# Four layers in one program: output projection folded into the value weights, shorter copies of the folded-in rows in two convolutions, and two sets of loads moved

## Chip, cores and metric

One core of a Trainium2 chip runs the whole program. The metric is the device time of one execution in microseconds. The core has five engines with a queue each: TensorE (PE, with its weight loads shown apart as PEld), VectorE (DVE), ScalarE (ACT), GpSimd (POOL) and SyncE (SP). SP and ScalarE issue the DMAs here. Numbers like L778 are lines of the kernel before.

## What is computed

The input is one image of 48 channels and 128x128 pixels (N = 16384 pixels). Four layers follow each other, each adding its result to its input after a group normalisation `_gn` (16 groups of 3 channels):

```
x = x + L0(_gn(x))   # attention over all 16384 pixels, one head of 48 channels
x = x + L1(_gn(x))   # four recurrent sweeps: down, up, right, left
x = x + L2(_gn(x))   # patch convolution with a product in the frequency domain
x = x + L3(_gn(x))   # state space scan over 4096 tokens of 192 values
```

- L0: a 1x1 convolution to 144 channels and a 3x3 depthwise one give q, k, v; q and k are normalised to length one; `softmax(q k^T * temperature) v` for every pixel; then a 48x48 projection of the result.
- L1: each row (then column) is its input plus a 5-tap convolution of the row before it, 508 steps that depend on each other.
- L2: a 1x1 convolution to 288 channels and a 3x3 depthwise one; q and k of each 8x8 patch are multiplied in the frequency domain, normalised over channels, multiplied by v and projected to 48 channels.
- L3: tokens of 2x2 pixels; B, C and the step sizes are matrix products of the tokens; a linear recurrence over the 4096 tokens for 192x192 states; output per token.

## The kernel before

Two image buffers, `xa` and `xb`, stay in on-chip memory (128 partitions, channels on partitions 0 to 47) and change roles between layers. `tile_kernel` (L1503) loads the image in 8 pieces on SP, then calls `attention`, `sweeps`, `patch_conv`, `image_out` and `scan`. Each takes its buffers from pools that it gives back at its end; a buffer that lies on given-back memory waits for that memory's last users.

The order on each engine is fixed when the program is built. `InOrder` (L38) keeps the operations of one wrapper in the order in which they are written; what is issued past it may be ordered otherwise by the builder. A queue's instructions are taken strictly in turn, so a DMA on SP that waits keeps those behind it waiting. Eight semaphores are shared by all DMAs in rotation, so a DMA is issued only when the one eight places before it has landed.

**Both convolutions** (L166 to L233, L741 to L818) fold the depthwise 3x3 kernel into the 1x1 weights (`packed_weights`, L100): a product of both for each of 9 taps, summed by matmuls. Partitions are packed so that three matmuls (one for each horizontal shift) cover most of it: partitions 0 to 47 (48 in the patch convolution, with a row of ones) hold image row y, partitions 64 on hold row y+1, and the gaps between hold a part of the channels of row y+2. The remaining channels of row y+2 are copied three times, with the three shifts, into a buffer `rest`, once at partition 0 and once at 64, and a fourth matmul takes those. Two neighbouring outputs (two halves of eight rows in attention, even and odd rows in the patch convolution) take the copy at 0 and the copy at 64, so that two small matmuls can lie side by side on TensorE. Each of the two copies holds all rows.

In attention a `band` is 16 rows: normalised by VectorE, one copy of the whole to the upper partitions (L181), two for the gaps (L183), six for `rest` (L191), all on SP, two bands in flight. In the patch convolution `fill` (L760) does the same for 8 rows with L765, L768 and L778, `rest` in a ring of three buffers; the first fill puts its `rest` copies on ScalarE's queue. TensorE works in groups g of 4 rows: `columns` (the three shifts), later `others` (the `rest` matmul), then the transforms, `turn`, `leave` and `count`.

**Attention's loop** (`attend`, L303). For each chunk of 512 queries (32 chunks), 64 steps: `scores` makes s = k^T q in four quarter matmuls on both halves of the keys, ScalarE exponentiates, `sums` adds v e into `acc` two steps later. Channel 32 of v is a column of ones, so `acc` also holds the softmax denominators. `Finish` copies `acc` out and adds the two halves (L361). At step 6 of the next chunk `result` multiplies by `proj` (L365), which also spreads the denominators over 48 partitions, and divides and adds the input. `attend_shifted` is for large temperatures and doesn't run here.

**Sweeps** load their weights `w` and `wi` (L573, L575) at their beginning. **`image_out`** (L1537) stores the image to `x3` in device memory in 8 pieces and forms the last normalisation's statistics; the scan reads `x3` back, for its first chunk in `first` (L1042), where ScalarE and VectorE then normalise it into `xn`. The scan itself runs over 4 chunks of 1024 tokens with 288 scans each on VectorE (L1478) and as many products on GpSimd (L1471).

Of the kernel before, what the change touches and what calls it, by code (L numbers as in the profile page):

```python
# [26 lines left out]
C = 48  # L27
H = W = 128
# [85 lines left out]
def attention(ctx, tc, xq, other, x1, const, ins):  # L114
# [11 lines left out]
    v = other[:, HALF:N].rearrange("p (t c) -> p t c", c=64)  # L126


    proj = kv.tile([128, 64 + C], F32, name="proj")
    nc.vector.memset(proj, 0.0)  # L130
    for b in (0, 64):
        nc.sync.dma_start(proj[b : b + GAP, 0:C], ins["l0_proj"])
        nc.vector.memset(proj[b + 32 : b + 33, 64:], 1.0)
    temp = kv.tile([128, 1], F32, name="temp")
# [8 lines left out]
    with ExitStack() as a:  # L143
# [8 lines left out]
        wt = packed_weights(nc, wp, "wt", ins["l0_w"], ins["l0_dw"], 192)  # L152

        for i in range(NQ):
            nc.vector.bn_stats(st[:, i, :], xq[0:C, i * CH : (i + 1) * CH])
# [5 lines left out]
        bands = [wp.tile([128, R + 2, S], F32, name=f"band{i}") for i in range(2)]  # L161
        rests = [wp.tile([128, R, S], F32, name=f"rest{i}") for i in range(2)]
        for t in bands + rests:
            nc.gpsimd.memset(t, 0.0)

        def band(b):  # L166

            t, e = bands[b % 2], rests[b % 2]  # L170
            first = b * R - 1
            lo, hi = max(first, 0), min(first + R + 2, H)
            normalise(
                nc,
                t[0:C, lo - first : hi - first, 1 : W + 1],
                rows(xq[0:C, lo * W : hi * W]),
                stats,
            )
            if b == NB - 1:
                nc.gpsimd.memset(t[0:C, hi - first : hi - first + 1, :], 0.0)  # L180
            nc.sync.dma_start(t[64 : 64 + C, 0 : R + 1], t[0:C, 1 : R + 2])  # L181
            for n in range(2):
                nc.sync.dma_start(  # L183
                    t[64 * n + C : 64 * n + 64, 0:R], t[16 * n : 16 * n + 16, 2 : R + 2]
                )
            flat = t.rearrange("c h w -> c (h w)")
            long = R * S - 2
            for n in range(2):
                for dx in range(3):
                    at = 64 * n + 16 * dx  # L190
                    nc.sync.dma_start(  # L191
                        e.rearrange("c h w -> c (h w)")[at : at + 16, 0:long],
                        flat[32:C, 2 * S + dx : 2 * S + dx + long],
                    )
            return t, e

        def conv(p, pv, te, y):
# [12 lines left out]
            def rest(out, n, c):  # L210
                at = 64 * n
                pe.matmul(
                    rows(out),
                    lhsT=wt[at : at + C, 3, c],
                    rhs=e[at : at + C, y + 4 * n : y + 4 * n + 4, 0:W],
                    start=False,
                    stop=True,
                )
# [16 lines left out]
        def take(t0, p, pv):  # L235
# [36 lines left out]
            nc.gpsimd.memset(k[kb + 32 : kb + 33, tk : tk + 2 * CH], 1.0)  # L272
            nc.gpsimd.memset(v[:, t0 // 128 : t0 // 128 + 8, 32:33], 1.0)
            return left
# [21 lines left out]
    with tc.If(small <= bits) as near:  # L296
        attend(tc, xq, k, v, x1, proj, absT, st, ins)
    with near.Else():
        attend_shifted(tc, xq, k, v, x1, proj, absT, ident, st, ins)


@with_exitstack
def attend(ctx, tc, xq, k, v, x1, proj, absT, st, ins):  # L303

# [45 lines left out]
    class Finish:  # L350


        def __init__(self, c, acc):
# [5 lines left out]
            act.copy(o, acc)  # L359
            self.o = sp.tile([128, CH], F32, name="osum")  # L360
            nc.vector.tensor_add(self.o, o[:, 0], o[:, 1])  # L361

        def result(self):
            p = ps_s.tile([128, 2, CH], F32, name="s")[0 : 64 + C, 0, :]
            pe.matmul(p, lhsT=proj, rhs=self.o, start=True, stop=True)  # L365
            y = sp.tile([64 + C, CH], F32, name="y")
            act.copy(y, p)
            rec = sp.tile([C, CH], F32, name="rec")
            nc.vector.reciprocal(rec, y[64 : 64 + C])  # L369
            nc.vector.tensor_mul(rec, y[0:C], rec)  # L370
            nc.vector.tensor_add(xq[0:C, self.cols], rec, self.xres)
            nc.vector.bn_stats(st[:, self.c, :], xq[0:C, self.cols])
            nc.sync.dma_start(x1[:, self.cols], xq[0:C, self.cols])
# [22 lines left out]
@with_exitstack  # L396
def attend_shifted(ctx, tc, xq, k, v, x1, proj, absT, ident, st, ins):

# [14 lines left out]
    for i in range(0, HALF, 2048):  # L413
        nc.vector.tensor_copy(k16[:, i : i + 2048], k[:, i : i + 2048])

    class Shift:
# [46 lines left out]
    class Finish:  # L463
# [10 lines left out]
        def result(self):  # L474
            p = ps_1.tile([128, CH], F32, name="pmisc")
            nc.tensor.matmul(p[0 : 64 + C], lhsT=proj, rhs=self.o, start=True, stop=True)
            rec = sp.tile([C, CH], F32, name="rec")
# [76 lines left out]
def sweeps(ctx, tc, xq, other, x1, const, ins):  # L554
# [15 lines left out]


    w = pool.tile([128, 3, 3, K], F32, name="w")
    nc.sync.dma_start(w, ins["l1_w"])  # L573
    wi = pool.tile([128, 3, K], F32, name="wi")
    nc.sync.dma_start(wi, ins["l1_wi"])  # L575
    mask = pool.tile([128, L], F32, name="mask")
# [118 lines left out]
@with_exitstack  # L695
def patch_conv(ctx, tc, xq, other, const, ins):

# [42 lines left out]


    K1 = C + 1
    SP = W + 2
# [8 lines left out]
    stats = group_stats(nc, wp, ps_f, const, name="f")  # L752
    flat = xp.rearrange("c h w -> c (h w)")
    rests = [wp.tile([128, RN, SP], F32, name=f"rest{i}") for i in range(3)]

    def rest(y):

        return rests[(y + 1) // RN % 3][:, (y + 1) % RN, 0:W]

    def fill(r, queue=nc.sync):  # L760
        inside = xp[0:64, 1 + r : 1 + RN + r, 1 : W + 1]
        nc.gpsimd.memset(inside[32:64], 1.0)
        normalise(nc, inside[0:C], rows(xq[0:C, r * W : (r + RN) * W]), stats)
        new = slice(r + 1, r + 1 + RN)
        nc.sync.dma_start(xp[64 : 64 + K1, r : r + RN, :], xp[0:K1, new, :])  # L765
        lo, hi = max(r - 1, 0), H if r + RN == H else r - 1 + RN
        for n in range(2):
            nc.sync.dma_start(  # L768
                xp[64 * n + K1 : 64 * n + 64, lo:hi, :],
                xp[M * n : M * n + M, lo + 2 : hi + 2, :],  # L770
            )
        e = rests[r // RN % 3].rearrange("c h w -> c (h w)")
        size = KR // 3
        long = RN * SP - 2
        for n in range(2):
            for dx in range(3):
                at = 64 * n + size * dx
                queue.dma_start(  # L778
                    e[at : at + size, 0:long],
                    flat[2 * M : K1, (r + 1) * SP + dx : (r + 1) * SP + dx + long],  # L780
                )
# [116 lines left out]
    def count(g):  # L898
        dve.bn_stats(const["st"][:, g, :], xq[0:C, g * CH : (g + 1) * CH])

    NG = H // G
    fill(0, act)
    fill(RN)
# [41 lines left out]
def scan(ctx, tc, x3, const, ins, out):  # L945
# [72 lines left out]
    def prepare(ci):  # L1018
# [9 lines left out]
        def first():  # L1028
# [6 lines left out]
            for part in range(NP):  # L1035
                us.append(ap.tile([C2, 2, L], F32, name="xn"))
                src = x3[:, part * NR * W : (part + 1) * NR * W].rearrange(
                    "c (i a w) -> a c i w", a=2, w=W
                )
                raw = rows(ct[0:C2, part, :])  # L1040
                for i in range(2):
                    nc.sync.dma_start(raw[i * C : (i + 1) * C], src[i])  # L1042
            for part, x in enumerate(us):
                xi = rows(ct[0:C2, part, :]).rearrange("c i (j b) -> c i j b", b=2)
                xo = x.rearrange("c b (i j) -> c i j b", j=64)
# [457 lines left out]
def tile_kernel(ctx: ExitStack, tc: tile.TileContext, ins: dict, out: bass.AP):  # L1503
# [4 lines left out]
    x1 = dram.tile([C, N], F32, name="x1")  # L1508
    x3 = dram.tile([C, N], F32, name="x3")
    with ExitStack() as image:  # L1510
        xp = image.enter_context(tc.tile_pool(name="image", bufs=1))

        xa = xp.tile([128, W * (W + 6)], F32, name="xa")
        xb = xp.tile([128, (H + 6) * (W + 6)], F32, name="xb")
        for i in range(0, N, 2048):
            nc.sync.dma_start(xa[0:C, i : i + 2048], ins["x"][:, i : i + 2048])
        attention(tc, xa, xb, x1, const, ins)
        sweeps(tc, xa, xb, x1, const, ins)
        patch_conv(tc, xb, xa, const, ins)
        image_out(tc, xb, x3, const)  # L1520
    scan(tc, x3, const, ins, out)
# [14 lines left out]
@with_exitstack  # L1536
def image_out(ctx, tc, xq, x3, const):  # L1537

    nc = tc.nc
    pool = ctx.enter_context(tc.tile_pool(name="io", bufs=1))  # L1540
    psum = ctx.enter_context(tc.tile_pool(name="io_ps", bufs=1, space=PSUM))
    for i in range(0, N, 2048):
        nc.sync.dma_start(x3[:, i : i + 2048], xq[0:C, i : i + 2048])
    token_stats(tc, pool, psum, const)
# [171 lines left out]
```

## Time and profile before

The median of three executions is 7664.13 us (7662.93 to 7669.04). The profiled execution took 7668.22 us; its span, from the first to the last instruction, is 7666.4 us.

| Stage | us from the start | length |
|---|---|---|
| image load, statistics, first band | 0 to 43 | 43 |
| attention: convolution | 43 to 254 | 211 |
| attention: loop over chunks | 254 to 3817 | 3563 |
| last result, statistics, first rows of the sweeps | 3817 to 3841 | 24 |
| sweeps | 3841 to 4508 | 667 |
| patch convolution, up to its second group | 4508 to 4550 | 42 |
| patch convolution, rest | 4550 to 4925 | 375 |
| store of the image, loads and first products of the scan | 4925 to 4941 | 16 |
| scan | 4941 to 7666 | 2725 |

Over the whole span TensorE is busy for 6186.0 us, ScalarE 4405.6, VectorE 3353.1, GpSimd 2793.6. These sums say little, because the stages have different limits; the stretches below are by stage. In lines of the timeline the first two numbers are start and length in us, then engine, line, operation, what is written and read with its shape, and how many instructions were merged; the bracket tells how long the engine stood idle before, and what ended that. L48 is the line of the `InOrder` helper, so such operations are told apart by their buffers.

### The profile page before, as it was taken

What the parts mean: (1) busy time and instruction counts of PE and PEld (TensorE: products, weight loads), DVE (VectorE), ACT (ScalarE), POOL (GpSimd) and SP (SyncE); (2) the same over time, 40 slices, a digit from 0 to 9 for tenths busy, and PEclk for the clock granted to TensorE, in tenths of its full rate; (3) what the DMA queues carried; (4) which work ended last, traced back from release to release, by engine and by line L of the source; (5) the groups of instructions that cost most, each with busy time, mean ns of one, the idle gap of its engine ahead of it and who ended that gap; (6) DMA issues with size and microseconds to landing.
All of it is one profiled execution on the core that took longest, in us unless ns stands there. A gap on an engine that the chain in (4) does not pass through costs nothing. (4 is left out here: it accounts for less than half of the span.)

```text
span 7666.4 us, 202951 instructions
## 1 busy us (share of the span) xinstructions
PE 6186.0 (81%) x93744; PEld 3145.7 (41%) x93744; DVE 3353.1 (44%) x2435; ACT 4405.6 (57%) x4864; POOL 2793.6 (36%) x573
## 2 busy tenths in 40 slices
PE   7999999999999999999988879745545555554555
PEld 2333333333333333333367755434434333434444
DVE  8300000000000000000022234489999999999998
ACT  2566666666666666666625003366666666666665
POOL 1000000000000000000000022299999999999998
PEclk9999999999999999999999999866767666776666
DMA  5000000000000000000000001166556566666776
GB/s 76 10 3 3 3 2 3 3 3 2 3 3 2 3 3 3 2 3 3 6 1 17 1 27 50 31 168 165 158 161 164 152 161 155 164 158 162 181 178 152
DMA packets 167594, 488.77 MB, mean 64 GB/s; under 512 B 33568, under 2 KB 51968, under 8 KB 163984
## 3 DMA queue, kind: packets, MB, share of 16 engines
q1 hardware_dynamic: 160584, 469.79, 24.4%
q8 instruction: 736, 12.06, 0.7%
q10 hardware_dynamic: 6152, 5.92, 0.3%
q14 instruction: 122, 1.00, 0.0%
HBM read 428.82 MB, written 22.02 MB: 59 GB/s over the span
## 5 line engine op out<-in xcount | busy, mean ns | idle before, releaser
L48 ACT ACTIVATE e<-s,absT 128x1024 f32<-128x1024 f32 x2048 | 2279.4, 1115 | 1215.1 <-PE s L48 1215.0
L1471 POOL TENSOR_TENSOR h<-du,bt 128x3072 f32<-128x3072 f32 (+1 forms) x386 | 2559.8, 6670 | 94.5 <-DMA du<-rep 77.4
L48 PE MATMUL s<-xa,xb 49*64 49x512 f32 x16384 | 2127.7, 589 | 10.6 <-DVE xb L266 10.6
L48 PE MATMUL acc<-e,xb 64*64 64x512 f32 x16384 | 2123.6, 588 | 0.0
L1478 DVE TENSOR_TENSOR_SCAN h<-dA,carry,h 128x1024 f32<-128x1024 f32 x864 | 1939.8, 2324 | 46.1 <-ACT dA L48 31.2
L48 ACT ACTIVATE dA<-dt,a 128x1024 f32<-128x1024 f32 x1152 | 1287.2, 1118 | 873.8 <-DVE h L1478 864.6
L48 PE MATMUL y<-h,cw 128*32 128x48 f32 x49152 | 892.0, 245 | 930.6 <-issue 486.6
L361 DVE TENSOR_TENSOR osum<-o 128x512 f32<-128x512 f32 x32 | 22.2, 693 | 3114.2 <-ACT o L48 3114.2
L593 POOL MEMSET xa<- 48x128 f32 x1 | 0.3, 324 | 3560.3 <-PE acc L48 3560.3
L48 PEld LDWEIGHTS y<-h,cw 128*32 128x32 f32 x49152 | 802.8, 139 | 1059.7 <-issue 650.7
L48 PEld LDWEIGHTS s<-xa,xb 49*64 49x64 f32 x16384 | 624.8, 132 | 1152.1 <-issue 603.7
L48 PEld LDWEIGHTS acc<-e,xb 64*64 64x64 f32 x16384 | 627.1, 132 | 1135.0 <-issue 1112.4
L1478 DVE TENSOR_TENSOR_SCAN h<-dA,h 128x1024 f32<-128x1024 f32 x288 | 636.1, 2270 | 45.9 <-ACT dA L48 34.9
L48 PE MATMUL yz<-ev,sel 128*8 128x48 f32 x4096 | 192.7, 260 | 288.1 <-ACT ev L48 283.1
L48 PEld LDWEIGHTS yz<-ev,sel 128*8 128x8 f32 x4096 | 162.4, 106 | 345.6 <-ACT ev L48 321.7
L657 PE MATMUL p<-xb,w 112*112 112x129 f32 x1524 | 236.4, 291 | 41.9 <-DVE xb L48 41.8
L657 PE MATMUL p<-xa,w 112*112 112x129 f32 x1524 | 232.2, 288 | 41.9 <-DVE xa L48 41.9
L678 POOL TENSOR_TENSOR xb<-xb,xa 48x2048 f32<-48x2048 f32 (+2 forms) x10 | 44.6, 4460 | 562.3 <-DVE xa L48 562.3
L657 PEld LDWEIGHTS p<-xb,w 112*112 112x112 f32 x1524 | 184.3, 179 | 93.8 <-DVE xb L48 93.8
L640 ACT COPY xa<-xb 48x128 f32<-48x128 f32 x256 | 107.4, 420 | 197.3 <-issue 138.8
L369 DVE RECIPROCAL rec<-y 48x512 f32<-48x512 f32 x32 | 107.1, 3348 | 257.7 <-ACT y L48 257.7
L657 PEld LDWEIGHTS p<-xa,w 112*112 112x112 f32 x1524 | 180.6, 176 | 93.3 <-DVE xa L48 93.3
(182 smaller groups left out, 3474.8 us busy)
## 6 DMA issues: line engine op xcount, KB each, us to landing
du<-rep SPq DMA_DIRECT2D x768, 256.0 KB
dt<-rep SPq DMA_DIRECT2D x768, 256.0 KB
rest<-xa SPq DMA_DIRECT2D x90, 77.0 KB
rest<-band SPq DMA_DIRECT2D x48, 129.9 KB
rep<-dd SPq DMA_DIRECT2D x24, 192.0 KB
yd<-ys ACTq DMA_DIRECT2D x256, 12.0 KB
band<-band SPq DMA_DIRECT2D x8, 414.4 KB
xa<-xa SPq DMA_DIRECT2D x16, 199.1 KB
```

The costliest lines, as they stand in the source:

```text
L48: ins = method(*args, **kwargs).ins
L361: nc.vector.tensor_add(self.o, o[:, 0], o[:, 1])
L369: nc.vector.reciprocal(rec, y[64 : 64 + C])
L593: nc.gpsimd.memset(b[64:K, lines, E + W - 1 : E + W], 0.0)
L640: nc.scalar.copy(u[at : at + C, :, y], t[0:C, E + h, E : E + W])
L657: nc.tensor.matmul(p, lhsT=w[0:K, which, i, :], rhs=state[0:K, 2 * i : 2 * i + L], start=False, stop=(i == 2),)
L678: nc.gpsimd.tensor_add(xr, xr, u[0:C, x : x + xr.shape[2], E : E + H].rearrange("c w h -> c h w"),)
L1471: nc.gpsimd.tensor_mul(h[:, p, ks], du.unsqueeze(1).to_broadcast([128, ks.stop - ks.start, LC]), r["bt"][:, ks],)
L1478: nc.vector.tensor_tensor_scan(h[:, p, k, :], dA, h[:, p, k, :], carry[:, i, k : k + 1] if ci else 0.0, ALU.mult, ALU.add,)
```

## The change

1. The value part of attention's weights is multiplied by the projection on chip, once: four transposes, a copy, four matmuls with `proj`, a copy back. `acc` then holds projected values. The ones in v fill channels 48 to 63, so the denominator lies on 16 partitions; the reciprocal is taken there and three small copies on SP bring it to 48 partitions. The matmul with `proj` leaves the loop.
2. In both convolutions each of the two copies in `rest` holds only the rows that its own matmuls read, without the columns at the border: 4 rows of 128 values in a copy of its own in attention (12 copies a band instead of 6), every second row in the patch convolution. The first fill there is split into 5 rows and 3 rows.
3. The sweeps' weights are loaded right behind the image.
4. The stores of `x3` are issued in `count`, every fourth group, from inside the patch convolution; for the first 8 groups the rows are also copied on chip to a buffer `x3_first` in the order in which the scan's first chunk wants them, and that chunk's four loads go.

```diff
-    proj = kv.tile([128, 64 + C], F32, name="proj")
+    proj = kv.tile([64, 64], F32, name="proj")
     nc.vector.memset(proj, 0.0)
-    for b in (0, 64):
-        nc.sync.dma_start(proj[b : b + GAP, 0:C], ins["l0_proj"])
-        nc.vector.memset(proj[b + 32 : b + 33, 64:], 1.0)
+    nc.sync.dma_start(proj[0:GAP, 0:C], ins["l0_proj"])
...
+        values = wt[:, :, 128:192]
+        turned = wp.tile([64, 4, 128], F32, name="turned")
+        pt = ps1.tile([128, 4, 2, 64], F32, name="pt").rearrange("c t n o -> c t (n o)")
+        for t in range(4):
+            pe.transpose(pt[0:64, t, :], values[:, t, :], ident)
+        act.copy(turned, pt[0:64])
+        pt = ps1.tile([128, 4, 2, 64], F32, name="pt")
+        for t in range(4):
+            pe.matmul(pt[:, t, 0, :], lhsT=turned[:, t, :], rhs=proj, start=True, stop=True)
+        act.copy(values, pt[:, :, 0, :])
...
-        rests = [wp.tile([128, R, S], F32, name=f"rest{i}") for i in range(2)]
+        rests = [wp.tile([128, R // 8, 4, W], F32, name=f"rest{i}") for i in range(2)]
...
+            two = t[32:C, 2:, :].rearrange("c (k n i) w -> c n k i w", n=2, i=4)
+            for i in range(R // 8):
+                for n in range(2):
+                    for dx in range(3):
+                        at = 64 * n + 16 * dx
+                        nc.sync.dma_start(e[at : at + 16, i], two[:, n, i, :, dx : dx + W])
...
-            nc.gpsimd.memset(v[:, t0 // 128 : t0 // 128 + 8, 32:33], 1.0)
+            nc.gpsimd.memset(v[:, t0 // 128 : t0 // 128 + 8, C:64], 1.0)
...
-            self.o = sp.tile([128, CH], F32, name="osum")
-            nc.vector.tensor_add(self.o, o[:, 0], o[:, 1])
+            both = sp.tile([128, CH], F32, name="both")
+            nc.vector.tensor_add(both, o[:, 0], o[:, 1])
+            second = sp.tile([64, CH], F32, name="second")
+            nc.vector.tensor_copy(second, both[64:128])
+            self.y = sp.tile([64, CH], F32, name="y")
+            nc.vector.tensor_add(self.y, both[0:64], second)
+
+            rec = sp.tile([64, CH], F32, name="rec")
+            nc.vector.reciprocal(rec[32:64], self.y[32:64])
+            self.rec = sp.tile([C, CH], F32, name="recs")
+            for i in range(0, C, 64 - C):
+                nc.sync.dma_start(self.rec[i : i + 64 - C], rec[C:64])
 
         def result(self):
-            p = ps_s.tile([128, 2, CH], F32, name="s")[0 : 64 + C, 0, :]
-            pe.matmul(p, lhsT=proj, rhs=self.o, start=True, stop=True)
-            y = sp.tile([64 + C, CH], F32, name="y")
-            act.copy(y, p)
-            rec = sp.tile([C, CH], F32, name="rec")
-            nc.vector.reciprocal(rec, y[64 : 64 + C])
-            nc.vector.tensor_mul(rec, y[0:C], rec)
-            nc.vector.tensor_add(xq[0:C, self.cols], rec, self.xres)
+            y = self.y[0:C]
+            nc.vector.tensor_mul(y, y, self.rec)
+            nc.vector.tensor_add(xq[0:C, self.cols], y, self.xres)
...
-    w = pool.tile([128, 3, 3, K], F32, name="w")
-    nc.sync.dma_start(w, ins["l1_w"])
-    wi = pool.tile([128, 3, K], F32, name="wi")
-    nc.sync.dma_start(wi, ins["l1_wi"])
+    w, wi = const["l1_w"], const["l1_wi"]
...
-    def fill(r, queue=nc.sync):
-        inside = xp[0:64, 1 + r : 1 + RN + r, 1 : W + 1]
+    def fill(r, first=0, end=RN, queue=nc.sync):
+
+        at = slice(1 + r + first, 1 + r + end)
+        inside = xp[0:64, at, 1 : W + 1]
         nc.gpsimd.memset(inside[32:64], 1.0)
...
+        nc.sync.dma_start(xp[64 : 64 + K1, r + first : r + end, :], xp[0:K1, at, :])
+        lo, hi = max(r - 1 + first, 0), H if r + end == H else r - 1 + end
...
         for n in range(2):
+            own = range(first + (first + n + 1) % 2, end, 2)
             for dx in range(3):
-                at = 64 * n + size * dx
+                to = 64 * n + size * dx
                 queue.dma_start(
-                    e[at : at + size, 0:long],
-                    flat[2 * M : K1, (r + 1) * SP + dx : (r + 1) * SP + dx + long],
+                    e[to : to + size, own.start // 2 : own.start // 2 + len(own), :],
+                    xp[2 * M : K1, r + 1 + own.start : r + 1 + end : 2, dx : dx + W],
                 )
...
     def count(g):
         dve.bn_stats(const["st"][:, g, :], xq[0:C, g * CH : (g + 1) * CH])
+        if g % 4 == 3:
+            new = slice((g - 3) * CH, (g + 1) * CH)
+            nc.sync.dma_start(x3[:, new], xq[0:C, new])
+            if g < 8:
+                own = xq[0:C, new].rearrange("c (i a w) -> a c i w", a=2, w=W)
+                for a in range(2):
+                    nc.sync.dma_start(rows(const["x3"][a * C : (a + 1) * C, g // 4]), own[a])
...
-    fill(0, act)
+    fill(0, 0, G + 1, act)
+    fill(0, G + 1)
     fill(RN)
...
-                for i in range(2):
-                    nc.sync.dma_start(raw[i * C : (i + 1) * C], src[i])
             for part, x in enumerate(us):
-                xi = rows(ct[0:C2, part, :]).rearrange("c i (j b) -> c i j b", b=2)
+                xi = rows(const["x3"][:, part, :]).rearrange("c i (j b) -> c i j b", b=2)
...
         for i in range(0, N, 2048):
             nc.sync.dma_start(xa[0:C, i : i + 2048], ins["x"][:, i : i + 2048])
+        for name in ("l1_w", "l1_wi"):
+            nc.sync.dma_start(const[name], ins[name])
         attention(tc, xa, xb, x1, const, ins)
         sweeps(tc, xa, xb, x1, const, ins)
-        patch_conv(tc, xb, xa, const, ins)
-        image_out(tc, xb, x3, const)
+        patch_conv(tc, xb, xa, x3, const, ins)
+        scan_stats(tc, const)
```

## The prediction

> **What bounds the kernel now.** I read the busy time by stages first (stretches cut at the stage changes), then the order of time inside each stage the diff touches, and last what the waits are put down to. In the stretches the columns after the length are busy TensorE, weight load, VectorE, ScalarE, GpSimd with instruction counts, then granted clock, DMA share, GB/s.
>
> ```profile
> 43.00:244.00 201.00, 200.45 (x640) 74.75 (x640) 178.64 (x143) 61.95 (x109) 18.66 (x31) 1.00 0.42 55
> 254.00:3817.00 3563.00, 3562.66 (x32830) 1260.33 (x32830) 189.10 (x156) 2323.53 (x2112) 1.27 (x2) 1.00 0.01 3
> 4508.00:4550.00 42.00, 11.64 (x38) 7.84 (x38) 17.78 (x29) 1.70 (x5) 3.17 (x5) 0.64 0.26 77
> 4550.00:4925.00 375.00, 353.60 (x1822) 205.50 (x1820) 154.54 (x319) 107.12 (x252) 95.84 (x96) 0.96 0.13 38
> 4941.00:7666.40 2725.40, 1471.77 (x54336) 1116.59 (x54334) 2598.69 (x1176) 1753.69 (x2084) 2573.71 (x392) 0.69 0.62 161
> ```
>
> Attention's convolution (43 to 244) and its loop (254 to 3817) are TensorE without a gap; the scan is VectorE and GpSimd; the patch convolution is TensorE with a start (4508 to 4550) in which it works 11.6 of 42 us. So cheaper copies give nothing where TensorE is full, a matmul less in attention gives all of itself, and the start of the patch convolution has room. The scan's body is not touched.
>
> **Value projection, attention loop.** Per chunk the loop has one foreign matmul:
>
> ```profile
> 375.63 1.05 PE L48 MATMUL s<-xa,xb 49*64 49x512 f32 x8
> 376.49 1.05 PE L48 MATMUL acc<-e,xb 64*64 64x512 f32 x8
> 377.48 1.11 PE L48 MATMUL s<-osum,proj 128*112 128x512 f32 x2
> 378.52 1.09 PE L48 MATMUL s<-xa,xb 49*64 49x512 f32 x8
> ```
>
> Without it s follows s by 1.72 us (the pairs from 3779.87 to 3814.27: 34.40 / 20); here 2.89, so its slot costs 1.17. The chunk period agrees: 111.28 us between these matmuls, 64 x 1.72 = 110.08, so 1.20. All but the last chunk have it inside the loop: 31 x 1.20 = **-37.2**. The new VectorE chain per chunk (add, copy, add, reciprocal 3.35) and three row copies in Finish lie beside a TensorE that waits for none of them: VectorE is busy 189 of 3563 us, SP issues two DMAs a chunk. ScalarE loses a 0.59 us copy and is not the bound (2324 of 3563).
>
> The last chunk lies open. Today from the last acc (3817.03) to the end of bn_stats (3826.51), 9.48 us, of which osum to reciprocal goes over matmul, y copy and their hand-overs: 3818.83 to 3820.95 = 2.12. New in that place: a 64x512 copy (no such row; between 0.36, the SBUF TENSOR_SCALAR of 128x512, and 0.69, the PSUM copy; I take 0.36, nearest in memory), an add (0.69), gaps 0.1: 1.15. After the reciprocal come three copies of 32 KB on SP: two issues of about 0.4 ahead of the third, which lands some 2.0 after its issue (the x1 store at 384.11 landed at 386.06); sum about 2.9. Net -1.0 + 2.9 = **+1.9** (bounds 0.5 and 4). Everything to the first sweep step shifts with it: VectorE reaches bn_aggr after its branch, ScalarE L602 waits for off.
>
> Building the new values: 4 transposes, 4 matmuls, 2 ScalarE copies, at about 13 to 31.5 us, when TensorE and ScalarE are idle but for the statistics. Cost 0 if proj has landed by 40 (first conv matmul 42.91).
>
> **Sweep weights with the image.** Their transfer now runs 3828 to 3830.3 by the stretch rows (DMA share 0.90 and 0.95), while the first sweep matmul starts at 3841.18, when the sixth L602 activation ends (3841.09). So removal gains 0. At the front they are issued on SP ahead of proj and temp. The image's last piece lands at 27.48, temp at 27.82; 672 KB took 2.2 us at 3828, so temp lands near 30.1. VectorE runs sgn (needs temp) at 29.45, ahead of the last bn_stats: **+0.8** (0 if sgn is ordered later, 1.2 at most).
>
> **Row copies, attention's convolution.** 6 copies of 130 KB per band become 12 of 32 KB. TensorE is full, the next band's rest is needed some 20 us after it is filled. First band: first conv matmul waits for the band copies (L183, landed 42.67), which stand ahead on SP; the rest matmul at 50.74 followed without a wait. **0**; if the 12 issues (0.5 each by the L1042 rows) were late, +2.
>
> **Row copies, patch convolution.** Here they bind at the start and once later:
>
> ```profile
> 4523.17 7.58 PE L48 MATMUL pc<-wt,xa 128*128 128x288 f32 x24 [10.04 <-DMA xa<-xa]
> 4547.23 2.26 PE L48 MATMUL pc<-wt,rest 57*128 57x288 f32 x6 [15.79 <-DMA rest<-xa]
> 4690.77 1.29 PE L48 MATMUL pc<-wt,rest 57*128 57x288 f32 x2 [2.79 <-DMA rest<-xa]
> ```
>
> The landing marks show why. A 19-row copy gives one mark besides the one at issue: it runs on one DMA engine. Its 19 packets of 4152 B start 0.158 us apart, 3.03 us a copy, and copies follow each other without a gap (4562.19, 4565.21, 4568.25). The band copy at 4514.68 has all its marks by 4518.4 but one, at 4522.19: its piece on that same engine, interleaved with rest pieces. A fill of 8 rows costs this engine 6 x 3.03 + 1.5 = 19.7, and two stand ahead of the first groups.
>
> After: 76 pieces of 512 B a copy. No SBUF row of 512 B exists. Packets of 4, 384, 4152 B take 9, 20-22, 161 ns, a line on which 512 is 27; the 512 B reads of x3 take 25-27 in the faster half, 49 in the median at the contended scan start. I take 27; ends 25 and 54 (their upper quartile). [...] But in the trace the fixed part of one copy lies under the next, so I take 6 x 76 x 0.027 + 1.5 = 13.8.
>
> Start, on that engine: first fill of 5 rows 0.9 + 285 x 0.027 = 8.6; its other 3 rows 0.6 + 171 x 0.027 = 5.2; second fill 13.8. From 4516.1 that ends near 4543.7. Columns start when the small band copies land, about 4518.7 instead of 4523.2; the first rest (ScalarE's queue, sharing the engine with SP's) is complete by 4531.5; the second group's columns then run, and its rest needs the second fill: 4543.7 against 4557.46. That is -13.7; a 3 us gap may drop the clock to half (the gap at 4687.9 did, for 6.8 us), which costs some 1.7: **-12** (bounds -18 and -4).
>
> The stall at 4690: the period of that group is 17.27 against 10.89. With fills of 13.8 per 21.8 us instead of 19.7 this one should not recur: **-6.4** (bounds -6.4 and +3). New on SP are 8 stores of x3 and 4 copies of its first rows. The stores exist today and were sent among the fills (4690.70, 4698.07); they and the 4 copies use 16 engines, under 1 us each. A store waits for leave of its last group; queued behind it are band and rest copies, which groups 2 to 3 iterations later need. 0 with 20 us cover; without it, the delay comes straight onto TensorE.
>
> **Scan's first rows.**
>
> ```profile
> 4932.51 2.09 SPq L1042 DMA_DIRECT2D ct<-x  x4
> 4935.85 0.44 ACT L48 ACTIVATE a<-a 128x288 f32<-128x288 f32 x1 [2.12 <-DMA a<-in_l_a_dram]
> 4938.22 2.27 ACT L48 ACTIVATE xn<-ct,so 96x1024 f32<-96x1024 f32 x1 [1.93 <-DMA ct<-x]
> 4940.54 9.85 PE L48 MATMUL dA<-xn,wdt 96*96 96x512 f32 x16 [10.47 <-ACT xn L48]
> ```
>
> The four loads go, but a's exponential stands ahead of xn on ScalarE and waits for its load till 4935.83, and that load waits as before for the last x3 store (4929.17). So xn moves from 4938.22 to about 4936.3: **-1.9**, not the 5 to 8 us that the loads seem to cost.
>
> **Sum.** -37.2 + 1.9 + 0.8 - 12 - 6.4 - 1.9 = -54.8. The profiled execution took 7668.2 us (span 7666.4): 7613. The runs' median is 7664.1, 4 lower, so **7610**.
>
> **Rivals.**
> - Patch convolution gives nothing: the stall moves to another group, since SP's order puts band copies and stores ahead of rest copies (as at 4673 to 4691). Then -37.2 + 1.9 + 0.8 - 1.9 = -36.4: 7628. For it: the stall came with the engine not full. Against: the start's stall is bytes on one engine. Chance 0.22, with all half-way cases above 7624.
> - Slower: the price of a 512 B piece. At p, a fill is 456 p + 1.5 us; over 44.5 ns it exceeds two groups (21.8) and the stage becomes DMA-bound. Gains are used up at 49 ns: 14 fills x (456 p - 20.3) + 912 (p - 0.027) = 13.7 + 36.4. At 54 ns: 14 x 4.3 + 10.9 at the start, -36.4 elsewhere: 7699. For it: the contended 49 ns median. Against: 25-27 uncontended. 0.04.
> - The projection's slot closes only half (TensorE meets another wait at the chunk's change): -18.6 instead of -37.2: 7628. Against: no wait stands at that place. 0.06.
> - That the projection is not gone from the loop: the diff takes the matmul out; no chance. Forecast case 7596 to 7624: 0.66; remainder 0.02.
>
> A difference under 0.2% (15 us) can't be told from none here. Faster 0.945, same 0.015, slower 0.04. The range 7596 to 7632 holds the first and nearly all of the second and third case.
>
> **What would show it.** Chunk period 110.08; no matmul from osum; last acc to bn_stats near 11.4 us; wait for rest at the start under 6 us and the second group's rest near 36 us after the sweeps' end (49 now); no 17 us group; 512 B packets near 27 ns; xn right behind a's exponential. Wrong if a new wait on rest, a store or the row copies appears on TensorE.

## The result and the profile after

The changed kernel takes 7616.98 us (median of 4 runs, 7611.93 to 7621.76); the kernel before, run beside it, 7666.06. The ratio is 0.9935, with an interval of 0.992 to 0.9951. The profiled execution took 7615.01 us, span 7613.2, against 7668.22 and 7666.4: 53.2 us less.

Three stretches of the changed kernel's span, in the columns of the stretches shown before, cut at its own stage changes:

```profile
252.00:3778.30 3526.30, 3525.85 (x32768) 1300.19 (x32768) 223.31 (x218) 2305.36 (x2081) 1.27 (x2) 1.00 0.02 4
3778.30:3817.00 38.70, 0.75 (x8) 0.60 (x5) 21.61 (x14) 9.76 (x10) 15.78 (x8) 0.54 0.03 7
4483.50:4533.00 49.50, 30.39 (x111) 19.62 (x112) 19.45 (x31) 3.71 (x10) 2.85 (x5) 0.72 0.25 72
```

The loop holds 32768 matmuls instead of 32830 in the stretch shown before (31 products with `proj`, two matmuls each, are gone), and lasts 3526 instead of 3563 us. But the second row, from the last `acc` to the first sweep matmul, is 38.7 us long, where the kernel before needed 24.15; VectorE is busy for 21.6 us of it and TensorE for 0.75. By stages, from the records of the two executions:

| Stretch | before | after | change | predicted |
|---|---|---|---|---|
| start to the first conv matmul | 42.91 | 42.57 | -0.3 | +0.8 |
| attention's convolution | 200.39 | 198.85 | -1.5 | 0 |
| loop, first s to last acc | 3562.69 | 3525.86 | -36.8 | -37.2 |
| last acc to first sweep matmul | 24.15 | 38.58 | **+14.4** | +1.9 |
| sweeps | 666.90 | 666.65 | -0.3 | 0 |
| patch convolution, statistics to last leave | 414.58 | 397.96 | -16.6 | -12 - 6.4 |
| last leave to first dA | 15.15 | 12.60 | -2.6 | -1.9 |
| scan, first dA to end | 2725.87 | 2716.36 | -9.5 | 0 |

Two rows are off: the tail of attention, and the scan, whose body the change does not touch. In the timeline of the changed kernel the tail reads:

```profile
3778.83 13.91 POOL L604 MEMSET xb<- 32x16512 f32 x1
3779.45 0.69 DVE L366 TENSOR_TENSOR both<-o 128x512 f32<-128x512 f32 x1 [97.35 <-ACT o L48]
3780.17 12.85 DVE L368 COPY second<-both 64x512 f32<-64x512 f32 x1
3793.05 0.69 DVE L370 TENSOR_TENSOR y<-both,second 64x512 f32<-64x512 f32 x1
3800.36 0.68 DVE L380 TENSOR_TENSOR y<-y,recs 48x512 f32<-48x512 f32 x1 [3.24 <-DMA recs<-rec]
```

The shift copy (`second`, from partitions 64 to 127 to 0 to 63) of the last chunk took 12.85 us. The changed kernel has 32 copies of this shape, with 422 ns as the median (shortest, median and longest, in ns):

```profile
L368 DVE COPY second<-both x32: 421/422/12847, 369.9 to 3780.2; 64x512 f32<-64x512 f32 x32
```

The last one begins 1.3 us after GpSimd's fill of `xb` with ones, the first work of the sweeps, and ends at 3793.02, 0.28 us after that fill (3792.74). The add ahead of it, with the same fill beside it, took its usual 0.69. No wait is shown: the whole 12.85 us count as busy, so the stretch's busy VectorE (21.61 us) is where the lost time hides. Beside one fill the copy, with one input, was long and the add, with two, was not. That the fill held the copy, and that the number of inputs decides, was the author's guess at this point and not yet shown.

### The profile page after: what moved, and what is told of

The parts are those of the page before. It is cut to its first block, busy times and chain, and to the rows that moved or that the text cites. A ratio compares the mean times of both kernels' runs of the same rounds, so it can differ in the third digit from the quotient of the medians.

```text
span 7613.2 us, 203122 instructions
## 1 busy us (share of the span) xinstructions
PE 6126.1 (80%) x93692; PEld 3179.7 (42%) x93692; DVE 3405.3 (45%) x2498; ACT 4389.0 (58%) x4835; POOL 2791.8 (37%) x574
## 3 DMA queue, kind: packets, MB, share of 16 engines
q1 hardware_dynamic: 175167, 466.19, 24.2%
## 4 chain that ended last, share of the span: by engine, by line
PE 60%; DVE 24%; issue 6%; POOL 3%; ACT 2%; DMA 2%; SPq 0%; DVEq 0%; ACTq 0%; POOLq 0%
PE s L48 23%; PE acc L48 23%; DVE h L1496 21%; PE p L672 6%; POOL h L1489 3%; PE pc L48 3%; PE y L48 3%; DVE xb L48 1%; DVE xa L48 1%; PE po L48 1%; DMA du<-rep 1%; PE f L48 1%; ACT dA L48 1%; PE pp L48 0%; ACT L48 0%
## 5 line engine op out<-in xcount | busy, mean ns | idle before, releaser
L366 DVE TENSOR_TENSOR both<-o 128x512 f32<-128x512 f32 x32 | 22.1, 692 | 3192.8 <-ACT o L48 3192.8
L48 PEld LDWEIGHTS s<-xa,xb 49*64 49x64 f32 x16384 | 650.5, 132 | 1123.2 <-issue 583.4
L48 PEld LDWEIGHTS acc<-e,xb 64*64 64x64 f32 x16384 | 649.7, 132 | 1112.4 <-issue 1089.5
L672 PE MATMUL p<-xb,l_w 112*112 112x129 f32 x1524 | 236.4, 291 | 41.8 <-DVE xb L48 41.7
L672 PE MATMUL p<-xa,l_w 112*112 112x129 f32 x1524 | 232.2, 288 | 41.8 <-DVE xa L48 41.8
L672 PEld LDWEIGHTS p<-xb,l_w 112*112 112x112 f32 x1524 | 184.3, 179 | 93.6 <-DVE xb L48 93.6
L672 PEld LDWEIGHTS p<-xa,l_w 112*112 112x112 f32 x1524 | 180.6, 176 | 93.2 <-DVE xa L48 93.2
L48 PE MATMUL pc<-wt,xa 128*128 128x288 f32 x768 | 199.7, 418 | 7.5 <-DMA xa<-xa 7.5
```

The costliest lines, as they stand in the source:

```text
L48: ins = method(*args, **kwargs).ins
L366: nc.vector.tensor_add(both, o[:, 0], o[:, 1])
L672: nc.tensor.matmul(p, lhsT=w[0:K, which, i, :], rhs=state[0:K, 2 * i : 2 * i + L], start=False, stop=(i == 2),)
```

## The experiments

Times and stretches in this part are those of one profiled execution each, unless a range or a ratio is given.

**The blocked copy.** Two edits, each leaving the other side as it is. The first asks whether a form with two inputs passes beside the same fill in the add's 0.69 us; the second, whether the copy waits for one GpSimd instruction or for all that GpSimd has to do. If for one, the copy was expected under 2.4 us with the fill cut, and the stretch from the last `acc` to the first sweep matmul near 28.

```diff
-            nc.vector.tensor_copy(second, both[64:128])
+            nc.vector.tensor_tensor(second, both[64:128], both[64:128], ALU.max)
```

> The changed kernel with the shift copy (second from both) written as the maximum of its input with itself, an operation with two on-chip inputs. [...] Then the operation takes about 0.69 us, last acc to first sweep matmul goes from 38.58 to about 26.5 us, and the profiled time from 7615 to about 7603. Rival one: reading partitions 64 to 127 into 0 to 63 is slow in itself at this place: 12.9 us stay, 38.6 stay. Rival two: the time is given back, since the first sweep rows wait for the end of GpSimd's fills: the operation is 0.69 but the stretch stays above 32.

```diff
-        nc.gpsimd.memset(b[32:64, lines, inside], 1.0)
+        n = lines.stop - lines.start
+        for i in range(lines.start, lines.stop, n // 8):
+            nc.gpsimd.memset(b[32:64, i : i + n // 8, inside], 1.0)
```

> The changed kernel with the copy as it is, and GpSimd's long fill of xb with ones cut into 8 (16 lines of it each, some 1.74 us). [...] Rival: GpSimd keeps VectorE out as long as it has work: 12 to 13 us again, 38.6 again. In the rival in which the copy itself is slow (its crossing of partitions), also 12.9.

The timeline of the first, with the two-input operation:

```profile
3777.77 13.91 POOL L604 MEMSET xb<- 32x16512 f32 x1
3779.11 0.69 DVE L368 TENSOR_TENSOR second<-both 64x512 f32<-64x512 f32 x1
```

and of the second, with the fill in pieces:

```profile
3779.29 1.82 POOL L606 MEMSET xb<- 32x2064 f32 x1
3780.57 0.82 DVE L368 COPY second<-both 64x512 f32<-64x512 f32 x1
3800.68 0.74 PE L649 MATMUL p<-xb,l_wi 112*112 112x129 f32 x2 [4.87 <-ACT xb L619]
```

With two inputs the operation crosses the same partitions under the same fill in 0.69 us; the stretch fell from 38.58 to 26.62 us, the profiled time to 7596.3 (7 less than expected; 3.0 of that lie in the sweeps, whose code is the same). With the fill cut, the unchanged copy took 0.82 us: it ended 0.28 us after the end of the running piece (3781.11), and GpSimd went on with further fills; the stretch is 22.0, the time 7598.6. So the crossing of partitions is not slow (0.69), the copy did not wait for all of GpSimd's work (0.82), and the time is not given back later (26.62 and 22.0 instead of 38.58): with the fill whole or cut, the unchanged copy ended 0.28 us after the one GpSimd instruction that was running when it began. Not every operation with one input is held: the reciprocal behind it ran beside the same fill in its usual 3.34 us (from 3780.55, in the first of the two runs).

The second edit gave 6 us more than expected (22.0 instead of about 28), and 4.6 more than the first. In the trace the first sweep matmul then starts 2.65 us after the start of the first normalising activation on ScalarE, instead of 7.18 (an activation takes 1.16, so after the second instead of the sixth). Why the matmul's wait depends on the fill's size stays open.

**The projection alone**: the kernel before with part 1 of the change only. Its core, of the hunks shown above:

```diff
-            self.o = sp.tile([128, CH], F32, name="osum")
-            nc.vector.tensor_add(self.o, o[:, 0], o[:, 1])
+            both = sp.tile([128, CH], F32, name="both")
+            nc.vector.tensor_add(both, o[:, 0], o[:, 1])
+            second = sp.tile([64, CH], F32, name="second")
+            nc.vector.tensor_copy(second, both[64:128])
...
```

> The kernel before with the value projection alone (part 1 of the change). Theory: it brings the loop's 37 us and all of the longer tail: first s to last acc 3525.9 instead of 3562.7, last acc to first sweep matmul 38.6 instead of 24.2, patch convolution (statistics to last leave) 414.6 and start of the scan as before; 7668.2 - 36.8 + 14.4 = 7646. Rival: the longer tail comes from another part (the sweep weights that stand in the image's memory from the start, so that GpSimd's fills begin earlier): tail 24 to 27, total about 7633.

The loop took 3525.3 us, the tail 38.57 with a copy of 12.85 again, the patch convolution 413.3, and the execution 7636.1. The tail belongs to part 1: the rival (sweep weights) fell. The total is 10 below the expected 7646, of which 7 lie in the scan (2718.9 instead of 2725.9), whose code is that of the kernel before.

**Three parts undone**: the weights' loads are back in `sweeps`, attention's `rest` copies and the scan's first loads are those of the kernel before.

```diff
     w, wi = const["l1_w"], const["l1_wi"]
+    nc.sync.dma_start(w, ins["l1_w"])
+    nc.sync.dma_start(wi, ins["l1_wi"])
...
-        rests = [wp.tile([128, R // 8, 4, W], F32, name=f"rest{i}") for i in range(2)]
+        rests = [wp.tile([128, R, S], F32, name=f"rest{i}") for i in range(2)]
...
+                for i in range(2):
+                    nc.sync.dma_start(raw[i * C : (i + 1) * C], src[i])
```

> The changed kernel with three parts undone: the sweeps' weights are loaded in the sweeps, attention's row copies hold all rows (6 a band), the scan's first rows are loaded from x3 (the stores of x3 stay where the change put them, and the buffer x3_first is gone). Each has its own stretch. Theory: last acc to first sweep matmul stays 38.6 (the weights were hidden, 0); first p to last pss in attention's convolution 200.4 instead of 198.9 (+1.5, the wait of the first band's second rest matmul is back); last leave to first dA 15.1 instead of 12.6 (+2.5); sum +4, profiled time about 7619. Rival for the scan's 2716.4 us (2725.9 before): they came with the buffer x3_first and the missing loads; then first dA to end is 2726 again and the sum +13.5. If they are the spread between executions, the length is anything between 2710 and 2730.

Tail 38.63; attention's convolution 200.50; last leave to first dA 14.34; time 7619.65. The first two are as expected: the weights were hidden, and the smaller copies are worth 1.6 us, at one place. In the timelines this is the first band's wait, in the kernel before and then in the changed kernel:

```profile
50.74 1.12 PE L48 MATMUL p<-rest,wt 48*128 48x512 f32 x2
52.15 1.09 PE L48 MATMUL p<-rest,wt 48*128 48x512 f32 x2 [0.29 <-issue]
```

```profile
50.23 1.13 PE L48 MATMUL p<-rest,wt 48*128 48x512 f32 x4
```

The second pair stood behind the last of six copies of 130 KB (landed 52.06), which the bracket puts down to "issue". This convolution took 197.9 to 199.5 us in the seven kernels with the small copies, 200.2 to 202.0 in the four with the large ones. The scan's first rows are worth 1.7 to 2.6 us. The scan's body took 2718.3 with the loads back and `x3_first` gone, so that rival fell too.

The pattern of the blocked copy stands at a second place of the changed kernel, though no run tests it there. With the first rows already on chip, VectorE's half of `xn` falls under a GpSimd fill:

```profile
4888.17 5.22 POOL L1032 MEMSET cw<- 128x6144 f32 x1 [8.51 <-DVE gn_rstd L87]
4889.16 5.13 DVE L1069 TENSOR_SCALAR xn<-x_first,so 96x1024 f32<-96x1024 f32 x1
```

With the loads back, the same operation starts after the fill and takes 1.22 us. Here it costs the first product nothing, since that waits for ScalarE's half.

**The patch convolution**: halved rows and the split of the first fill, one at a time.

```diff
-    rests = [wp.tile([128, RN // 2, W], F32, name=f"rest{i}") for i in range(3)]
+    rests = [wp.tile([128, RN, SP], F32, name=f"rest{i}") for i in range(3)]
...
-                    e[to : to + size, own.start // 2 : own.start // 2 + len(own), :],
-                    xp[2 * M : K1, r + 1 + own.start : r + 1 + end : 2, dx : dx + W],
+                    e[to : to + size, first * SP : first * SP + long],
+                    flat[2 * M : K1, (r + 1 + first) * SP + dx : (r + 1 + first) * SP + dx + long],
```

> The changed kernel with full-row copies (19 packets of some thousand bytes) in the patch convolution's rest, the split of the first fill into 5 and 3 rows kept; so that it fits, the buffer x3_first is gone too and the scan's first rows are loaded from x3. Theory, from the one DMA engine that carries all rest copies: first fill 12.3 + 7.4 us, second 19.7, so the second group's rest comes 49 us after the end of the sweeps, as in the kernel before (36 with half the rows), and the later stall is back: statistics to last leave 411 to 417 us instead of 398. Rival: the split of the first fill brings the gain, and the bytes do not matter: 398 to 404 us.

```diff
-    fill(0, 0, G + 1, act)
-    fill(0, G + 1)
+    fill(0, queue=act)
```

> The changed kernel with half the rows in rest, but the first fill in one piece of 8 rows. Theory: the engine has the same bytes to carry, so the second group's rest comes about 36 us after the end of the sweeps as now; only the first group's comes later, 25 to 29 us instead of no wait at 21: statistics to last leave 397 to 401 us instead of 398. Rival (the split brings the gain): 406 us or more.

TensorE's timeline at the start, the second group's wait for `rest`: of the changed kernel (with what follows it),

```profile
4519.52 1.30 PE L48 MATMUL pc<-wt,rest 57*128 57x288 f32 x2 [6.20 <-DMA rest<-xa]
...
4524.72 8.19 PE L48 MATMUL pc<-wt,xa 128*128 128x288 f32 x24
...
4536.60 6.09 PE L48 MATMUL pc<-wt,xa 128*128 128x288 f32 x24
```

with full rows,

```profile
4535.11 1.30 PE L48 MATMUL pc<-wt,rest 57*128 57x288 f32 x2 [13.42 <-DMA rest<-xa]
```

and without the split:

```profile
4508.07 1.21 PE L48 MATMUL pc<-wt,rest 57*128 57x288 f32 x6 [0.87 <-DMA rest<-xa]
...
4518.98 0.72 PE L48 MATMUL pc<-wt,rest 57*128 57x288 f32 x2 [2.52 <-DMA rest<-xa]
```

From the end of the sweeps the pair comes after 36.0 us, 50.5 with full rows and 36.1 without the split; statistics to last leave 397.96, 411.59 and 396.65. The bytes of these copies decide (50.5 against 36.0), the split is worth nothing (36.1). Around that wait the granted clock is at half for 13.65 us (4515.3 to 4529.0), and 24 matmuls take 8.19 instead of 6.09. The row of that stretch has the clock as 0.51, the third number from the end:

```profile
4515.00:4529.00 14.00, 8.56 (x27) 4.25 (x28) 0.96 (x1) 1.20 (x2) 0.00 (x0) 0.51 0.16 41
```

One expectation failed: with full rows the late stall did not come back; all later periods were 10.89 us. Two accounts: the stores of `x3` stood elsewhere on SP, or TensorE was later and so had room. The kernel before with the stores in `count` and nothing else:

```diff
+        if g % 4 == 3:
+            new = slice((g - 3) * CH, (g + 1) * CH)
+            nc.sync.dma_start(x3[:, new], xq[0:C, new])
...
-    for i in range(0, N, 2048):
-        nc.sync.dma_start(x3[:, i : i + 2048], xq[0:C, i : i + 2048])
```

> The kernel before with one edit: the 8 stores of x3 are issued in count, every fourth group, as in the changed kernel, instead of behind the patch convolution. The copies of rest keep all their rows and the first fill stays whole. Theory one (order on SP, from the run with full rows, in which no late group was long): the late stall (a group period of 17.27 us near 4690, 10.89 else) came from the order of the band copies, stores and rest copies on SP, so it goes with the stores' place alone: no group over 12 us behind the start, statistics to last leave about 408 us instead of 414.6. Theory two (the prediction's: bytes on one engine): the long group stays, 414 to 415 us. The start is that of the kernel before under both: the second group's rest 49 us after the end of the sweeps.

The stall stayed, as theory two has it (patch convolution 413.87, one period of 16.67):

```profile
4691.88 1.30 PE L48 MATMUL pc<-wt,rest 57*128 57x288 f32 x2 [1.96 <-DMA rest<-xa]
```

The margins show how near each kernel is to a wait. Time from the landing of a fill's last `rest` copy to the matmuls that need its first row, for fills 2 to 9, in us:

| Kernel | fill 2 | 3 | 4 | 5 | 6 | 7 | 8 | 9 |
|---|---|---|---|---|---|---|---|---|
| before | 1.3 | 3.3 | 4.7 | 4.6 | 0.7 | **0.1** | 1.0 | 3.1 |
| stores in count | 1.2 | 3.1 | 4.7 | 4.6 | 1.6 | **0.1** | 1.1 | 4.3 |
| full rows, split | 4.6 | 6.6 | 8.4 | 8.5 | 7.0 | 3.6 | 2.1 | 4.1 |
| changed kernel | 11.8 | 20.7 | 27.5 | 28.9 | 28.2 | 29.9 | 29.8 | 30.0 |

At 0.1 TensorE waited (2.8 us in the kernel before, 2.0 with the stores in `count`). With full rows and the split, TensorE's third group starts 63.2 us after the sweeps instead of 59.2, and these 4 us alone would hide the wait of 2.8 us in the dip at fills 6 to 8. They are not all: without its wait the kernel before would stand at -2.7 for fill 7, so full rows with the split have 6.3 us more there, and what gave the other 2.3 is not known; the order on SP is a candidate. Half the rows give 30 us. That the later start was the main cause is read from this table and not shown; no run shifted TensorE alone.

**A better start.** Two edits, each with the cut fill and without the two-input operation. First, 16 partitions and 3 instead of 19:

```diff
-                queue.dma_start(
-                    e[to : to + size, own.start // 2 : own.start // 2 + len(own), :],
-                    xp[2 * M : K1, r + 1 + own.start : r + 1 + end : 2, dx : dx + W],
-                )
+                for lo, hi in ((0, 16), (16, size)) if r <= RN else ((0, size),):
+                    queue.dma_start(
+                        e[to + lo : to + hi, own.start // 2 : own.start // 2 + len(own), :],
+                        xp[2 * M + lo : 2 * M + hi, r + 1 + own.start : r + 1 + end : 2, dx : dx + W],
+                    )
```

> The changed kernel with two edits: GpSimd's fill with ones cut into 8 as before in this study, and in the first two fills of the patch convolution each 19-partition copy of rest sent as one of 16 partitions and one of 3. Theory: a copy of 16 partitions spreads over 16 DMA engines, so nothing is queued on a single engine; the second group's rest comes when its issues are through, some 27 to 31 us after the end of the sweeps instead of 36, no wait and no slower clock: statistics to last leave 385 to 391 us instead of 398, last acc to first sweep matmul 22; in all about 7588 to 7593, ratio to the kernel before 0.990. Rival one: the 12 more issues on SP take as long as the single engine did (1.3 us an issue, with the eight semaphores): 396 to 400 us. Rival two: the copy of 3 partitions still queues on one engine behind others: gain under 3 us.

SP's queue and TensorE in that run:

```profile
4475.38 9.24 SPq L797 DMA_DIRECT2D rest<-xa  x12
4487.17 8.74 SPq L797 DMA_DIRECT2D rest<-xa  x12
4497.16 1.30 PE L48 MATMUL pc<-wt,rest 57*128 57x288 f32 x2 [5.29 <-DMA rest<-xa]
```

Rival one held. A copy of the second fill now lands 1.8 to 2.2 us after its issue begins, but twelve issues take 8.74 us, one right behind the other: the limit is now SP, no longer the landings one behind the other (1.9 us apart in the second fill of the changed kernel). The pair comes 34.5 us after the sweeps, the patch convolution takes 396.1; the whole 7596.29 us, ratio 0.9906 [0.989, 0.9923], mostly from the cut fill. Second, the one row that is needed goes ahead of the other seven:

```diff
-    fill(RN)
+    fill(RN, 0, 1)
+    fill(RN, 1)
```

> The changed kernel with GpSimd's fill with ones cut into 8, and the second fill of the patch convolution split into its first row and the other 7: the second group needs of that fill only the first row. Theory: what holds the second group is that this row's copies stand behind others in SP's queue and on the one engine; sent ahead they land about 28 to 30 us after the end of the sweeps, the wait of 6.2 us and most of the time at half clock go, the third group's rest starts at 40 to 44 us instead of 49.3, statistics to last leave 388 to 392 us instead of 398, in all 7588 to 7592, ratio to the kernel before about 0.990. Rival: the wait moves to the third group, whose rest is then 6 issues later on SP: 396 to 400 us.

```profile
4493.68 1.24 PE L48 MATMUL pc<-wt,rest 57*128 57x288 f32 x8
4497.45 6.09 PE L48 MATMUL pc<-wt,xa 128*128 128x288 f32 x24
4503.46 0.75 PE L48 MATMUL pc<-wt,rest 57*128 57x288 f32 x2
```

In this timeline all eight matmuls of the second group's `rest` follow each other with no bracket, 28 us after the sweeps, the next columns run at full clock (6.09), and the third group's `rest` starts at 37.8 instead of 49.3. The patch convolution took 389.74, the tail 22.0, and the whole **7590.11 us** (7586.35 to 7590.93), ratio to the kernel before 0.9901 [0.9885, 0.9918]. This interval lies just below the changed kernel's 0.992 to 0.9951, each taken against the kernel before run beside it: it beats both kernels.

## Why the prediction was right, and where it was wrong

The time was forecast at 7610 and came at 7617.0, with the loop as its main term. But the sum hit closer than its terms, and that is partly luck: the tail cost 12.5 us more than forecast, and the scan, whose code is untouched, was 9.5 shorter in the profiled execution.

- **Loop**, -37.2: right (-36.8); `proj_alone` shows it by itself. The slot of 1.17 to 1.20 us closed almost wholly.
- **Attention tail**, +1.9, bounds 0.5 and 4: wrong, +14.4. The step that failed is "a 64x512 copy (no such row; between 0.36 ... and 0.69 ...; I take 0.36)". Its own price is 0.42, near what was taken; what was left out is what runs beside it. The last chunk was named as the one that lies open, but not that GpSimd starts the sweeps' 13.91 us fill in that very gap. The sign "last acc to bn_stats near 11.4 us" came as 24.2. Without the block the tail is 26.6 (+2.5), inside the bounds, so the rest of that step (three row copies, the hand-overs) was sized well.

The trace of before had both halves of this step. The same fill begins in the gap, where the two-input `osum` ran beside it unhindered:

```profile
3817.12 13.92 POOL L589 MEMSET xb<- 32x16512 f32 x1 [1.21 <-PE acc L48]
3818.14 0.69 DVE L361 TENSOR_TENSOR osum<-o 128x512 f32<-128x512 f32 x1 [94.81 <-ACT o L48]
```

And a one-input VectorE operation that else takes 0.38 took 0.92, and 1.29 at 132.46, beside a GpSimd fill of 0.94 or 0.95; it ended 0.28 us after the fill both times, as the copy did:

```profile
82.98 0.94 POOL L272 MEMSET xb<- 1x1024 f32 x1 [1.26 <-DVE xb L266]
83.29 0.92 DVE L258 TENSOR_SCALAR nrm<-nrm 128x512 f32<-128x512 f32 x1 [0.42 <-ACT nrm L48]
```

- **Start**, +0.8: -0.3. The late `temp` held nobody; VectorE runs `sgn` at 30.83, after the statistics (29.89).
- **Sweep weights**, 0: right. **Attention's copies**, 0: -1.5 to -1.6, since one pair of matmuls did wait for the first band's copies; the prediction read "followed without a wait" from the first pair alone.
- **Patch start**, -12: -9.9 at the third group (59.2 to 49.3). The arrival and what sets it, the bytes, were right: 512 B packets took 27 ns in the median as estimated, the rows came 36.0 us after the sweeps (35.6 forecast). The term that was mis-sized is the clock, put at 1.7 us: arrival gained 13.4, of which 3.5 went again in the half-clock stretch; the wait was 6.2 us, where the sign had said under 6. A fixed part of one copy was not shown by itself: 76 pieces at 27 ns are 2.05 us, a copy landed 1.9 us behind the one before (the last 2.3), and the six of the second fill landed within 9.9 us (4509.53 to 4519.39).
- **Late stall**, -6.4: right in size (in three executions with full rows and an unsplit first fill this period was 15.4 to 17.3 us) and, by the margins, in cause.
- **Scan start**, -1.9: -2.6, right: `xn` follows the exponential of `a`, as the timeline of the changed kernel shows.

```profile
4894.29 0.44 ACT L48 ACTIVATE a<-a 128x288 f32<-128x288 f32 x1 [2.04 <-DMA a<-in_l_a_dram]
4894.64 2.15 ACT L48 ACTIVATE xn<-x_first,so 96x1024 f32<-96x1024 f32 x1
4896.84 0.40 PEld L48 LDWEIGHTS dA<-xn,wdt 96*96 96x96 f32 x2 [7.99 <-ACT xn L48]
```

- **Scan**, 0: the two profiled executions differ by 9.5 us, but that is not shown to be the change. With the first rows loaded as before, the stretch took 2710.8 to 2726.2 us in five executions of this study; with them from the chip 2714.2 to 2719.0 in six. Leaving the scan out, the profiled executions differ by 43.7 us, where the prediction had 54.8: the gap of 11.1 is the tail's 12.5 less 1.4 from the other rows. What sets the scan's length from run to run stays open.

## What to carry to other kernels

When an operation is moved into a gap, price it with what the other engines do in that gap: here a one-input VectorE copy that met a long GpSimd fill lasted until the fill's end (12.85 us instead of 0.42), and that shows as busy time, not as a wait. Cutting the fill at the stage change cured it here (0.82), and so did a two-input form of the copy (0.69). Where several copies feed a stage, ask which row is needed first and send that alone; spreading them over more issues only moved the bound to the queue that issues (12 issues in 8.74 us).

## What the runs showed of the hardware

- A VectorE copy of 0.42 us took 12.85 beside one GpSimd fill of 13.91, in all five kernels that keep both as they are; the two-input form beside the same fill took 0.69. Two shorter one-input operations of the kernel before were held as well (0.92 and 1.29 instead of 0.38), while a third of their form (at 170.91) took 0.40 beside a fill of 1.63, and reciprocals took their usual 3.34 and 3.35.
- A copy of 19 partitions left one landing mark besides the one at its issue, with pieces of 512 B (27 ns each in the median at the start of the stage, a copy every 1.9 us) as with 4152 B (161 ns, 3.03 us). A copy of 16 partitions in attention left 16 landing marks. Cutting 19 into 16 and 3 won 1.5 us for the second group's pair (34.5 after the sweeps instead of 36.0): SP took 0.73 us an issue (12 in 8.74).
- At the start of the patch convolution, waits of TensorE for `rest` of 2.5, 5.3 and 6.2 us (without the split, with 16 and 3 partitions, changed kernel) came ahead of 24 column matmuls that took 7.81, 7.97 and 8.19 us instead of 6.09; in the changed kernel the granted clock was 0.5 for 13.65 us there. With one row ahead no wait behind the first columns was over 1.4 us, the column matmuls took 6.09, and the clock was 1.00 (4486 to 4520).
